# Cross-attention with image prompts: moving the context, prompt-value and input loads from the sync queue to GpSimd's queue

## The chip, the cores and the metric

The kernel runs on one core of a Trainium2 chip. The core has TensorE (PE in the profile) for matrix products, VectorE (DVE), ScalarE (ACT) and GpSimd (POOL) for everything else, and SyncE (SP), which here only issues DMAs. Each engine works through its own queue of instructions in order and meets the others through semaphores. A DMA is started by an instruction in the queue of one of these engines, and the bytes are then moved by 16 DMA engines that the core's queues share. The metric is the time of one execution on the device, in microseconds; a time is a median of several runs.

## What is computed

For each of 8 batch items, 112 positions of 320 channels attend with 20 heads of 16 channels to a context of 375 rows of 512 features. The first 371 rows are text, the last four are image prompts. All data is float32. The reference, cut to what matters:

```python
text_ehs = encoder_hidden_states[:, :-NUM_TOKENS]      # 371 rows
ip_ehs = encoder_hidden_states[:, -NUM_TOKENS:]        # 4 rows
q = heads(hidden_states @ W_q)
k_t = heads(text_ehs @ W_k); v_t = heads(text_ehs @ W_v)
probs_t = softmax(einsum('bhsd,bhtd->bhst', q, k_t) * attn_scale)
text_out = einsum('bhst,bhtd->bhsd', probs_t, v_t)
k_ip = heads(ip_ehs @ W_k_ip); v_ip = heads(ip_ehs @ W_v_ip)
qsem = l2norm(einsum('bhst,bte->bhse', probs_t, text_ehs))
sem = einsum('bhse,bne->bhsn', qsem, l2norm(ip_ehs))
fused = einsum('bhsd,bhnd->bhsn', q, k_ip) * attn_scale + SEM_SCALE * sem
probs_ip = softmax(fused) * spatial_mask[None, None, :, None]
ip_out = einsum('bhsn,bhnd->bhsd', probs_ip, v_ip)
out = (text_out + ip_out) @ W_out + b_out + residual
```

## The kernel before

**Steps and pairs.** The 20 heads of a batch item are five groups of four. A step is one group of one batch item, 40 steps in all. After a prologue the first step runs alone (`alone`), then the steps run two at a time: `pair(n - 1)` multiplies the steps `n - 1` and `n`, and `behind(n)` follows with the projections that later batches need. In the code, `one` and `two` are the two steps of a pair. The last batch has its own ending.

**What a step does.** Scores (L662) go to PSUM; VectorE takes their negated maxima (L675), ScalarE the exponentials `p` (L679) and a copy of the prompts' logits (L681). SyncE's queue sends `p` to the buffer `xg` in four DMAs (L686), one for each head. VectorE transposes `xg` in 32 x 32 blocks into `xgT` (L698), and TensorE multiplies `xgT` with `u` in 12 blocks (L710). `u` holds the Gram matrix of the context beside the values. Its Gram part comes from `ug` by DMAs on SyncE's queue (L488), its value part comes by DMAs through DRAM (L573, L582) to `vr`, and from there by a GpSimd copy for each step and each third of the context (`placed`, L629). VectorE multiplies the products by `p` and sums them (L763). `finish` and its pieces then do the prompts' softmax, the output projection and the store of one batch item, with GpSimd at L809 and L845 to L851.

**Contexts.** A context is transposed by VectorE from `ct` into `ctxT` (L402) in three parts; after the last part GpSimd copies the prompts' four columns in (`prompts_behind`, L390), and the Gram matmuls (L474) read them. `ct` has two buffers, so the context of batch b goes where that of batch b - 2 was. From batch 2 on, `load_ctx` first lets GpSimd clear one block of `ct` (L141); then come four DMAs of 32 x 11 rows of 512 bytes (L143) and four of 19 rows (L148), all on SyncE's queue. `load_next` calls it. It stands at the end of `behind(n)` where the second step of the pair is group 0 of an even batch (loading that batch's number plus 2) or group 4 of an even batch (plus 3).

**Prompt values and inputs.** `prompt_values` (L591) fetches one batch's four value rows from DRAM, repeated over 112 partitions, by one DMA on SyncE's queue. `x` comes in three DMAs on that queue: item 0 in the prologue, items 1 to 4 at L1194 in the first `behind`, items 5 to 7 at L1234 in the second.

**The order.** The order of the work on every engine is written out by hand: an instruction waits behind whatever was emitted before it on its engine. The SyncE queue therefore issues loads, `xg`, `u`, `vr` and `vd` transfers and stores in the order of the code. GpSimd's queue has the copies, clearings and products named above, and, once in the first `behind`, four DMAs (two for `w_out`, one each for the mask and the bias).

Of the kernel before, what the change touches and what calls it, by code (L numbers as in the profile page):

```python
# [20 lines left out]
def kernel(  # L21
# [14 lines left out]
    nc = tc.nc  # L36
# [24 lines left out]
    NG = H // GROUP  # L61
# [73 lines left out]
    def load_ctx(b):  # L135
        ct = io.tile([P, NT, E], F32, tag="ct", name=f"ct_{b}")
        if b >= LEAD:

            v = ct.rearrange("p c e -> p (c e)").rearrange("p (j f) -> p j f", f=P)
            full = TT // RG  # L140
            nc.gpsimd.memset(v[:, full, :], 0.0)  # L141
            for a in range(QN):
                nc.sync.dma_start(  # L143
                    v[a * RG : (a + 1) * RG, :full, :],
                    ehs[b, : full * RG, a * P : (a + 1) * P].rearrange("(j i) f -> i j f", i=RG),
                )
            for a in range(QN):
                nc.sync.dma_start(  # L148
                    v[a * RG : a * RG + TT - full * RG, full, :],
                    ehs[b, full * RG : TT, a * P : (a + 1) * P],  # L150
                )
            return v
        for c in range(NT):
            rows = min(P, T - c * P)
            some = rows - rows % 16
            nc.sync.dma_start(ct[:some, c, :], ehs[b, c * P : c * P + some, :])
            if some < rows:
                nc.sync.dma_start(ct[some:rows, c, :], ehs[b, c * P + some : c * P + rows, :])
        return ct
# [203 lines left out]
    def load_next(b):  # L363
        if 2 <= b < B:
            loaded[b] = load_ctx(b)
# [222 lines left out]

    def prompt_values(b):

        nc.sync.dma_start(  # L591
            st[b]["vip"].rearrange("p n h d -> p (n h d)"),
            vipd[b * NIP : (b + 1) * NIP, :].rearrange("n c -> (n c)").partition_broadcast(S),
        )
# [30 lines left out]
    def placed(b, g, chunks=range(NT)):  # L625

        s = st[b]
        for c in chunks:
            nc.gpsimd.tensor_copy(  # L629
                region(b, c)[:, :, UV - c * P :], s["vr"][:, c * QN : (c + 1) * QN, g, :]  # L630
            )
# [481 lines left out]
    def pair(n):  # L1113

        one, two = steps[n], steps[n + 1]
        b, g = one
        tags = ("mm", "sc") if b % 2 and g == NG - 1 else ("sc", "mm")
        ends = (BLK - 2, BLK - 1)

        products_in(b, g, ("qd",) * GROUP)  # L1120
        for j in range(BLK - 2):
            product(b, g, j, range(GROUP))
            if j < 2:
                heads = (HIGH, LOW)[j]
                coming_scores(n + LEAD, heads, tags[j])
                coming_probabilities(n + LEAD, heads)
            if j == 1:
                transposed(*two, BLK // 2, BLK)
            if j % QN == QN - 1:
                placed(*two, (j // QN,))  # L1130
        products_in(*two, (tags[1],) * 2 + (tags[0],) * 2)
        for there, here in ((HIGH, LOW), (LOW, HIGH)):
            product(*two, 0, there)
            for j in ends:
                product(b, g, j, here)
        del st[b]["xT", g]
        placed(*two, (NT - 1,))
        moved(b, g)
        if g > 1:
            turned(b + 2)  # L1140
        if b % 2 and g in (0, NG - 1):
            f(b - 1 - (g == 0))
        if g in (1, 2):
            f(b - 1, 3 - g)
        reduced(b, g)
        value_sums(b, g)

        b, g = two
        for j in range(1, BLK - 2):
            product(b, g, j, range(GROUP))  # L1150
            if j == 4:
                coming_scores(n + 1 + LEAD, HIGH, "qd")
                coming_probabilities(n + 1 + LEAD, HIGH)
            if j == 7:
                coming_scores(n + 1 + LEAD, LOW, "qd")
                coming_probabilities(n + 1 + LEAD, LOW)
        for heads in (HIGH, LOW):
            for j in ends:
                product(b, g, j, heads)
        del st[b]["xT", g]  # L1160
        moved(b, g)
        if one in ((b, 2), (b, 3)):
            turned(b + 2, 1 + (one == (0, 3)))

    def moved(b, g):

        nb = b + 1
        if b % 2 == 0:
            if g in (1, 2):
                gram_to_groups(nb, (g - 1,))  # L1170
            if g == 3:
                todo = [lambda: gram_to_groups(nb, (3,)), lambda: values_to_groups(nb)]
                for move in reversed(todo) if nb == B - 1 else todo:
                    move()
        else:
            if g in (0, 1):
                gram_to_groups(nb, (g,))
            if g == 2:
                values_to_groups(nb, 0, 2)

    def behind(n):

        b, g = steps[n]
        nb = b + 1
        two = steps[n + 1 : min(n + 3, len(steps) - NG + 1)]

        def tr(i):
            if i < len(two):
                transposed(*two[i], 0, BLK // (1 + i))

        if b % 2 == 0 and g == 0:
            if n == 0:
                turn[:] = ["sc", "mm", "qd", "mm"]
                nc.sync.dma_start(x_sb[:, 1:5, :], x[1:5].rearrange("b s c -> s b c"))  # L1194
            else:
                turn[:] = ["qd"] * 4 + ["mm"]
                k(b)
                f(b - 1)
                if b - 1 < B - 2:
                    prompt_values(b - 1)  # L1200
            if n:
                gr(nb)
            tr(0)
            gr(nb, 2)
            if n:
                f(b - 1)
            else:
                run(("pp",), prompt_projections)
            v(nb)
            tr(1)  # L1210
            if n:
                f(b - 1, 2)
            load_next(b + 2)
            if n == 0:
                load_channels(nc.gpsimd, wo_sb, w_out)
                nc.gpsimd.dma_start(sm_sb, smask.unsqueeze(1))
                nc.gpsimd.dma_start(bias_sb, b_out.partition_broadcast(S))
        elif b % 2 == 0 and g == 2:
            turn[:] = ["qd"] * (6 + (b == 0)) + ["mm"]
            gram_to_groups(nb, (2,))  # L1220
            if b == 0:
                run(("pp",), None)
            k(nb)
            q(nb, 3)
            tr(0)
            v(nb)
            q(nb)
            v(nb)
            if b == 0:
                run(("pp",), None)  # L1230
            tr(1)
            values_to_dram(nb, nc.sync)
            if b == 0:
                nc.sync.dma_start(x_sb[:, 5:, :], x[5:].rearrange("b s c -> s b c"))  # L1234
        elif b % 2 == 0 and nb < B - 1:
            turn[:] = ["qd"] * (4 + (b > 0)) + ["mm", "mm"]
            turned(b + 2)
            q(nb)
            if b > 0:
                f(b - 1)  # L1240
            else:
                run(("t", b), lambda: prompt_logits(b))
            k(nb)
            tr(0)
            if b > 0:
                f(b - 1)
            gr(nb + 1, 3)
            tr(1)
            if b > 0:
                f(b - 1)  # L1250
            load_next(b + 3)
            f(b)
            prompt_values(b)
        elif b % 2 == 0:
            turn[:] = ["qd"] * 4 + ["mm"]
            q(nb, 2)
            f(b - 1)
            k(nb)
            nc.scalar.preload_act_table(AF.Sqrt)
            tr(0)  # L1260
            f(b - 1, 2)
            prompt_values(b)
            f(b, 2)
        elif g == 1:
            turn[:] = ["qd"] * 4 + ["mm"]
            gram_to_groups(nb, (2,))
            q(b)
            k(b)
            k(nb)
            tr(0)  # L1270
            f(b - 1)
            v(nb)
            tr(1)
            v(nb)
            f(b - 1, 3)
            values_to_dram(nb, nc.sync, 0, 2)
            if b == B - 3:
                prompt_values_by_head()
        else:
            turn[:] = ["qd"] * 3 + ["sc"]  # L1280
            v(nb)
            f(b - 1)
            values_to_dram(nb, nc.sync, 2)
            tr(0)
            k(nb)
            f(b - 1, 2)
            tr(1)
            gram_to_groups(nb, (3,))
            values_to_groups(nb, 2)
        assert not turn, (b, g, turn)  # L1290
# [21 lines left out]
    b = B - 1  # L1312
# [116 lines left out]
```

## Time and profile before

| | us |
|---|---|
| runs | 425.0, 419.88, 420.75 |
| median | 420.75 |
| the profiled execution, its own time | 422.32 |
| its span in the profile | 420.6 |

| DMA queue (page of the profile) | packets | MB | share of 16 engines |
|---|---|---|---|
| q1, issued by SyncE | 57054 | 62.32 | 59.1% |
| q0, issued by GpSimd | 192 | 0.55 | 0.7% |

The second table is part 3 of the page. A line of engine groups names the source line, the engine, the operation and "output<-input", then the count, the busy time and the mean of one in ns, and the idle time just before with what ended it. In a timeline a line gives the start and the length in us, and in brackets the idle time before and its releaser. The letters q behind an engine (SPq, POOLq) mean its queue of instructions. In the chain of waits, a line gives the start and length of a stretch of the chain that ended last. In a table of stretches each engine has its busy time and, in brackets, its number of instructions; then come the granted TensorE clock, the DMA share and GB/s. The granted clock of TensorE was 0.997 over this execution.

### The profile page before, as it was taken

To read this page: it belongs to the slowest core of one execution; us is meant where nothing else is said; L and a number is where in the kernel's file an instruction comes from. 1 tells how busy PE (TensorE), PEld (TensorE's weight loads), DVE (VectorE), ACT (ScalarE), POOL (GpSimd) and SP (SyncE) were. 2 spreads that over 40 slices of the span, in tenths; PEclk is the share of its full clock that TensorE was granted. 3 is DMA by queue.
4 is the path that set the end of the run, shared out by engine and by line. 5 is a ranking of instruction groups with operands and counts; after the bars stand their busy time and mean duration, and the time that the engine had idled before them with its cause. 6 is when DMAs were issued, how large, how long until landed. Compare 5 with 4: busy or idle time off the path is not lost.

```text
span 420.6 us, 13818 instructions
## 1 busy us (share of the span) xinstructions
PE 413.4 (98%) x5505; PEld 316.4 (75%) x5505; DVE 322.3 (77%) x685; ACT 185.9 (44%) x634; POOL 115.0 (27%) x277
## 2 busy tenths in 40 slices
PE   8999999999999999999999999999999999999995
PEld 8766686878677786878686877778877878786893
DVE  4055777878888886886888896896887997879975
ACT  3263333324633643424553464333543464346773
POOL 4303310031161342012061235102025136005560
PEclk9999999999999999999999999999999999999998
DMA  8677986778555556577644576575656344676310
GB/s 249 170 195 224 182 168 169 174 183 193 146 160 131 162 137 168 139 166 169 173 122 127 149 172 156 140 171 152 174 136 164 96 121 129 158 167 195 91 42 27
DMA packets 58001, 64.63 MB, mean 154 GB/s; under 512 B 19016, under 2 KB 51760, under 8 KB 57938
## 3 DMA queue, kind: packets, MB, share of 16 engines
q1 hardware_dynamic: 57054, 62.32, 59.1%
q8 instruction: 43, 0.70, 0.8%
q10 hardware_dynamic: 692, 0.89, 0.7%
q0 software_dynamic: 192, 0.55, 0.7%
q14 instruction: 20, 0.16, 0.1%
HBM read 19.04 MB, written 5.22 MB: 58 GB/s over the span
## 4 chain that ended last, share of the span: by engine, by line
PE 91%; DVE 4%; DMA 2%; ACT 1%; POOL 1%; issue 0%; SPq 0%; DVEq 0%; POOLq 0%
PE ps_qd L710 43%; PE ps_v L543 15%; PE ps_k L512 10%; PE ps_g L474 7%; PE ps_s L662 6%; PE ps_q L344 4%; DMA xg<-p 2%; PE ps_o L865 2%; DVE xgT L698 1%; PE ps_g L444 1%; PE ps_c L414 1%; PE ps_w L431 1%; PE ps_kv L280 1%; PE ps_k L503 1%; DVE p L763 1%; POOL shared L752 1%
## 5 line engine op out<-in xcount | busy, mean ns | idle before, releaser
L710 PE MATMUL ps_qd<-u,xgT 32*112 32x40 f32 (+11 forms) x3840 | 217.1, 351 | 1.1 <-DVE ob L871 0.4
L710 PEld LDWEIGHTS ps_qd<-u,xgT 32*112 32x112 f32 x3840 | 179.8, 172 | 38.1 <-issue 6.2
L698 DVE STREAM_TRANSPOSE xgT<-xg 128x768 f32<-128x768 f32 (+1 forms) x63 | 122.9, 1972 | 10.5 <-DMA xg<-p 10.4
L679 ACT ACTIVATE p<-ps_s,nmx 112x371 f32<-112x371 f32 x160 | 85.8, 585 | 61.6 <-DVE nmx L675 61.3
L675 DVE TENSOR_REDUCE nmx<-ps_s 112x1 f32<-112x371 f32 x160 | 77.1, 535 | 34.3 <-PE ps_s L662 32.2
L763 DVE CUSTOM_DVE_ANT_0 p<-ps_qd,p 112x371 f32<-112x371 f32 x150 | 72.5, 539 | 16.5 <-ACT pvs L737 11.1
L629 POOL COPY u<-vr 128x64 f32<-128x64 f32 x120 | 26.8, 237 | 192.3 <-PE ps_qd L710 111.7
L543 PE MATMUL ps_v<-wv_sb,ctxT 128*128 128x384 f32 (+1 forms) x192 | 63.8, 479 | 0.3 <-ACT kT L519 0.3
L662 PE MATMUL ps_s<-kT,qm 32*112 32x375 f32 (+1 forms) x320 | 60.4, 486 | 0.0
L543 PEld LDWEIGHTS ps_v<-wv_sb,ctxT 128*128 128x128 f32 x192 | 35.3, 190 | 21.2 <-ACT kT L519 1.2
L512 PE MATMUL ps_k<-ctxT,wk_sb 128*128 128x371 f32 x136 | 45.8, 481 | 0.0
L737 ACT COPY pvs<-ps_qd 112x21 f32<-112x21 f32 x150 | 21.8, 199 | 52.3 <-DVE ss L763 49.8
L512 PEld LDWEIGHTS ps_k<-ctxT,wk_sb 128*128 128x128 f32 x136 | 24.6, 190 | 13.4 <-ACT ctxT L424 0.5
L474 PE MATMUL ps_g<-ctxT 128*32 128x119 f32 (+11 forms) x672 | 33.3, 344 | 0.0
L474 PEld LDWEIGHTS ps_g<-ctxT 128*32 128x32 f32 x672 | 25.9, 109 | 7.4 <-issue 4.2
L662 PEld LDWEIGHTS ps_s<-kT,qm 32*112 32x112 f32 x320 | 27.2, 171 | 4.8 <-ACT pvs L737 0.5
L550 ACT COPY vext<-ps_v 128x384 f32<-128x384 f32 (+1 forms) x24 | 11.2, 466 | 37.1 <-PE ps_v L543 37.0
L681 ACT COPY ipl<-ps_s 112x4 f32<-112x4 f32 x140 | 24.1, 172 | 0.0
L353 DVE TENSOR_SCALAR qm<-ps_q,emask 128x224 f32<-128x224 f32 (+1 forms) x25 | 8.9, 393 | 17.1 <-PE ps_q L344 17.1
L460 ACT ACTIVATE ug<-ps_g 128x375 f32<-128x375 f32 (+2 forms) x24 | 9.1, 378 | 28.5 <-PE ps_g L474 14.5
L519 ACT COPY kT<-ps_k 128x371 f32<-128x371 f32 x17 | 8.0, 469 | 30.4 <-PE ps_k L512 30.4
L402 DVE STREAM_TRANSPOSE ctxT<-ct 128x512 f32<-128x512 f32 x18 | 19.1, 1066 | 0.0
(158 smaller groups left out, 308.8 us busy)
## 6 DMA issues: line engine op xcount, KB each, us to landing
xg<-p SPq DMA_DIRECT2D x158, 162.3 KB
u<-ug SPq DMA_DIRECT2D x128, 99.0 KB
ct<-in_ctx_dram SPq DMA_DIRECT2D x24, 176.0 KB
vip<-vipd SPq DMA_DIRECT2D x7, 560.0 KB
vr<-vd SPq DMA_DIRECT2D x20, 120.0 KB
vd<-vext SPq DMA_DIRECT2D x14, 160.0 KB
vd<-vext SPq DMA_DIRECT2D x28, 40.0 KB
ct<-in_ctx_dram SPq DMA_DIRECT2D x4, 256.0 KB
```

Of the source, the lines that this page charges most:

```text
L474: nc.tensor.matmul(ps[p * RG : (p + 1) * RG, s0 : T - t0], ctxT[:, e, t0 + q * RG : t0 + (q + 1) * RG], ctxT[:, e, t0 + s0 : T], start=(e ...
L512: nc.tensor.matmul(ps[:, :TT], wk_sb[:, e, i * P : (i + 1) * P], s["ctxT"][:, e, :TT], start=(e == 0), stop=(e == NE - 1),)
L543: nc.tensor.matmul(ps[:, :w], ctxT[:, e, c * P : (c + 1) * P], wv_sb[:, e, :w], start=(e == 0), stop=(e == NE - 1),)
L629: nc.gpsimd.tensor_copy(region(b, c)[:, :, UV - c * P :], s["vr"][:, c * QN : (c + 1) * QN, g, :])
L662: nc.tensor.matmul(ps[:S, :w], qm[a * RG : (a + 1) * RG, i, r, j * S : (j + 1) * S], s["kT"][a * RG : (a + 1) * RG, i, :w], start=True, st ...
L675: nc.vector.tensor_reduce(nmx, ps[:S, :TT], AX.X, ALU.max, negate=True)
L679: nc.scalar.activation(p, ps[:S, :TT], AF.Exp, bias=nmx)
L681: nc.scalar.copy(s["ipl"][:, groups[g][a], :], ps[:S, TT:T])
L698: nc.vector.transpose(xT[:, j : j + n].rearrange("p j (k q) -> p q j k", q=QN), xg[:, :, j * RG : (j + n) * RG].rearrange("p q (j k) -> p ...
L710: nc.tensor.matmul(banks[a][:S, j * RG : UW], xT[a * RG : (a + 1) * RG, j, :S], region(b, c)[a * RG : (a + 1) * RG, p, q * RG :], start=(j ...
L737: nc.scalar.copy(s["pvs"][:, h, :], ps[:S, TT:UW])
L763: nc.vector.tensor_tensor_reduce(out=p, in0=ps[:S, :TT], in1=p, scale=1.0, scalar=0.0, op0=ALU.mult, op1=ALU.add, accum_out=s["ss"][:, h : ...
```

## The change

The eight DMAs of a context from batch 2 on, the prompt values and the x loads after the first item are issued by GpSimd instead of SyncE. `load_next` leaves `behind` and stands within `pair`, between the first step's last products and the second step's remaining ones, right after the third `placed` copy of the second step. The contexts 2, 3, 5 and 7 are thereby issued about half a pair later in the order than before, 4 and 6 earlier: within the pair before the place where they stood. The bytes, their layout and every other instruction stay as they are. The weights, contexts 0 and 1 and the first x item stay on SyncE's queue.

```diff
@@ -140,12 +140,12 @@
             full = TT // RG
             nc.gpsimd.memset(v[:, full, :], 0.0)
             for a in range(QN):
-                nc.sync.dma_start(
+                nc.gpsimd.dma_start(
                     v[a * RG : (a + 1) * RG, :full, :],
                     ehs[b, : full * RG, a * P : (a + 1) * P].rearrange("(j i) f -> i j f", i=RG),
                 )
             for a in range(QN):
-                nc.sync.dma_start(
+                nc.gpsimd.dma_start(
                     v[a * RG : a * RG + TT - full * RG, full, :],
                     ehs[b, full * RG : TT, a * P : (a + 1) * P],
                 )
@@ -588,7 +588,7 @@
     def prompt_values(b):
 
-        nc.sync.dma_start(
+        nc.gpsimd.dma_start(
             st[b]["vip"].rearrange("p n h d -> p (n h d)"),
             vipd[b * NIP : (b + 1) * NIP, :].rearrange("n c -> (n c)").partition_broadcast(S),
         )
@@ -1135,6 +1135,8 @@
                 product(b, g, j, here)
         del st[b]["xT", g]
         placed(*two, (NT - 1,))
+        if (b, g) == (0, 1) or b % 2 and g in (0, NG - 1):
+            load_next(b + 2 + g // (NG - 1))
         moved(b, g)
         if g > 1:
             turned(b + 2)
@@ -1191,7 +1193,7 @@
         if b % 2 == 0 and g == 0:
             if n == 0:
                 turn[:] = ["sc", "mm", "qd", "mm"]
-                nc.sync.dma_start(x_sb[:, 1:5, :], x[1:5].rearrange("b s c -> s b c"))
+                nc.gpsimd.dma_start(x_sb[:, 1:5, :], x[1:5].rearrange("b s c -> s b c"))
             else:
                 turn[:] = ["qd"] * 4 + ["mm"]
                 k(b)
@@ -1210,7 +1212,6 @@
             tr(1)
             if n:
                 f(b - 1, 2)
-            load_next(b + 2)
             if n == 0:
                 load_channels(nc.gpsimd, wo_sb, w_out)
                 nc.gpsimd.dma_start(sm_sb, smask.unsqueeze(1))
@@ -1231,7 +1232,7 @@
             tr(1)
             values_to_dram(nb, nc.sync)
             if b == 0:
-                nc.sync.dma_start(x_sb[:, 5:, :], x[5:].rearrange("b s c -> s b c"))
+                nc.gpsimd.dma_start(x_sb[:, 5:, :], x[5:].rearrange("b s c -> s b c"))
         elif b % 2 == 0 and nb < B - 1:
             turn[:] = ["qd"] * (4 + (b > 0)) + ["mm", "mm"]
             turned(b + 2)
@@ -1248,7 +1249,6 @@
             tr(1)
             if b > 0:
                 f(b - 1)
-            load_next(b + 3)
             f(b)
             prompt_values(b)
         elif b % 2 == 0:
```

## The prediction

> **What bounds the kernel now.** I read the page first, for the busy shares and the chain of work that ended last; then that chain in order of time, for the length of each stretch of the loop; then the timelines of VectorE, SyncE's queue and GpSimd around the context loads.
>
> ```profile
> PE 413.4 (98%) x5505; PEld 316.4 (75%) x5505; DVE 322.3 (77%) x685; ACT 185.9 (44%) x634; POOL 115.0 (27%) x277
> ...
> PE 91%; DVE 4%; DMA 2%; ACT 1%; POOL 1%; issue 0%; SPq 0%; DVEq 0%; POOLq 0%
> ```
>
> TensorE is busy for 98% of the span and makes 91% of the last chain; SyncE's queue makes none of it. So freeing that queue shortens nothing by itself. It can only remove places where TensorE stands still or runs thin because an `xg<-p` transfer came late. The steady loop shows how much there is of that, since every second batch repeats the same work. Pairs of groups begin with ten matmuls of L710:
>
> ```profile
> 89.14 1.15 PE ps_qd L710 x10
> ...
> 110.30 1.15 PE ps_qd L710 x10
> ...
> 167.28 1.15 PE ps_qd L710 x10
> ...
> 188.36 1.15 PE ps_qd L710 x10
> ...
> 208.38 1.15 PE ps_qd L710 x10
> ...
> 265.36 1.15 PE ps_qd L710 x10
> ...
> 307.86 1.15 PE ps_qd L710 x10
> ```
>
> The pair of batch 3, groups 0 and 1, takes 208.38 - 188.36 = 20.02 us. The same pair of batch 1 takes 110.30 - 89.14 = 21.16, which is 1.14 more. From 265.36 to 307.86 there are two pairs in 42.50 us; the same two took 208.38 - 167.28 = 41.10 two batches earlier, so 1.40 is lost there. These 2.5 us are all that the comparison of equal pairs shows to be recoverable. What went wrong stands on VectorE:
>
> ```profile
> 91.02 1.57 DVE L698 STREAM_TRANSPOSE xgT<-xg 128x768 f32<-128x768 f32 x1 [3.04 <-DMA xg<-p]
> ...
> 92.75 1.89 DVE L675 TENSOR_REDUCE nmx<-ps_s 112x1 f32<-112x371 f32 x4
> ...
> 205.37 1.58 DVE L698 STREAM_TRANSPOSE xgT<-xg 128x768 f32<-128x768 f32 x1
> ...
> 209.98 1.89 DVE L675 TENSOR_REDUCE nmx<-ps_s 112x1 f32<-112x371 f32 x4
> ...
> 285.75 1.59 DVE L698 STREAM_TRANSPOSE xgT<-xg 128x768 f32<-128x768 f32 x1 [1.86 <-DMA xg<-p]
> ```
>
> In both slow places VectorE waited for `xg<-p`. The reader should keep one exchange rate from these rows: the maxima (L675) began 92.75 - 89.14 = 3.61 us into the slow pair, and 209.98 - 208.38 = 1.60 into a pair that lost nothing. So 2.0 us of delay on VectorE cost 1.14 on TensorE, and about 0.86 was absorbed.
>
> **Part by part: SyncE's queue.** The change takes 48 context issues, 7 of prompt values and 2 of x off it.
>
> ```profile
> L143 SPq DMA_DIRECT2D ct<-in_ctx_dram x24: 411/465/1696, 43.0 to 284.5; - x24
> L148 SPq DMA_DIRECT2D ct<-in_ctx_dram x24: 224/281/2425, 46.8 to 288.5; - x24
> ```
>
> ```profile
> 183.01 2.05 SPq L143 DMA_DIRECT2D ct<-in_ctx_dram  x4
> 189.46 1.23 SPq L148 DMA_DIRECT2D ct<-in_ctx_dram  x4
> ...
> 191.14 3.54 SPq L686 DMA_DIRECT2D xg<-p  x4
> ...
> 198.86 4.02 SPq L686 DMA_DIRECT2D xg<-p  x4
> ```
>
> By the medians the context issues are 24 x 0.465 + 24 x 0.281 = 17.9 us of that queue, and L148 also holds it until GpSimd has cleared the block (183.01 + 2.05 to 189.46 here). Yet the next `xg<-p` went out only at 191.14, after the last of these at 190.69 and after the prompt values. It follows the probabilities of the pair that began at 188.36, so it has its own reason to be no earlier. I count nothing for the shorter queue here.
>
> At 281.37 it is different: the four `xg<-p` before the load of context 7 had been issued by then, and the transposes could start only at 285.75, 4.4 us later, against 205.37 - 202.88 = 2.5 where no context is on the move.
>
> ```profile
> 277.71 3.66 SPq L686 DMA_DIRECT2D xg<-p  x4
> ```
>
> Context 7 goes out straight behind it. Moving it into the next pair should give back the 1.40. The 1.14 of batch 1 can be due to the queue itself, since in the pair before it one x load is removed:
>
> ```profile
> 73.56 1.56 SPq L1234 DMA_DIRECT2D x_sb<-in_x_dram  x1
> ```
>
> It could give all of 1.14 or nothing; I take half, 0.6. Gains: 2.0 us, between 0 and 2.5.
>
> **GpSimd's queue.** Its own price for an issue has four rows:
>
> ```profile
> L118 POOL DMA_DIRECT2D wo_sb<-in_L_xattn_W_out_dram x1 | 0.9, 918 | 0.0
> ...
> L1216 POOL DMA_DIRECT2D sm_sb<-in_fside_S_dram x1 | 0.6, 554 | 0.0
> L1217 POOL DMA_DIRECT2D bias_sb<-in_L_xattn_b_out_dram x1 | 0.5, 546 | 0.0
> L119 POOL DMA_DIRECT2D wo_sb<-in_L_xattn_W_out_dram x1 | 0.5, 534 | 0.0
> ```
>
> By the code these move 256, 112, 112 and 64 contiguous rows. From 112 rows to 256 the price grows by 0.372 us, 2.6 ns a row. A large context DMA has 32 x 11 = 352 rows, so about 0.918 + 96 x 0.0026 = 1.17 us; a small one has 19 rows, 0.53. An estimate from these rows: 4 x 1.17 + 4 x 0.53 = 6.8 us per context, 7.0 with the clearing. From below it is 8 x 0.53 + 0.2 = 4.4; from above, if all of 918 ns is rows, 352 x 3.6 ns = 1.26 and 7.4. I take 7.0, nearest to the 256-row case. Prompt values cost seven times 0.55 and the two x loads (448 and 336 rows) 1.4 and 1.1. Together 6 x 7.0 + 3.9 + 2.5 = 48 us go onto an engine that has 115.0 busy in 420.6; average room is plenty. What counts is who is queued behind the issues:
>
> ```profile
> 55.01 0.24 POOL L629 COPY u<-vr 128x64 f32<-128x64 f32 x1 [1.30 <-PE ps_qd L710]
> ...
> 132.23 0.24 POOL L629 COPY u<-vr 128x64 f32<-128x64 f32 x1 [2.58 <-DMA vr<-vd]
> 134.39 0.20 POOL L390 COPY ctxT<-ipnT 128x16 f32<-128x16 f32 x1 [1.92 <-DVE ctxT L402]
> ...
> 194.96 0.24 POOL L629 COPY u<-vr 128x64 f32<-128x64 f32 x1 [1.59 <-PE ps_qd L710]
> ...
> 228.85 0.24 POOL L629 COPY u<-vr 128x64 f32<-128x64 f32 x1 [1.15 <-DMA vr<-vd]
> ```
>
> ```profile
> 139.36 4.64 PE ps_g L474 x71
> ...
> 237.44 4.64 PE ps_g L474 x71
> ```
>
> The new place is right behind the third L629 copy of a pair. For contexts 3, 5 and 7 (the place is 195.20 in batch 3) the next three copies and a small one (0.9 us) wait behind the issues, and TensorE needs them at 208.38: room for 12.3 us. For contexts 4 and 6 L390 waits behind them, and the Gram matmuls read its columns: 139.36 - 132.47 - 0.20 leaves 6.7 us, and 237.44 - 229.09 - 0.20 leaves 8.15. So 7.0 us are hidden everywhere but at context 4, which I charge 0.3 us. From above the 7.4 would cost 0.7. The place adds no long wait: the buffer's last reader finished pairs ago, and the prompt values' buffer is freed by GpSimd itself. x is not read before the next pair.
>
> Context 2 is now issued later, from 55.25 to 62.3, and its first reader is L402:
>
> ```profile
> L402 DVE STREAM_TRANSPOSE ctxT<-ct x18: 1005/1056/1127, 74.1 to 330.8; 128x512 f32<-128x512 f32 x18
> ...
> wo_sb<-in_L_xattn_W_out_dram POOLq DMA_DIRECT2D x1, 320.0 KB, 9.9
> ```
>
> Even at 9.9 us to landing it is there at 72.2, ahead of 74.1. The others have at least as long a lead, a full pair.
>
> **The transfers.** The bytes stay, but they move beside other transfers:
>
> ```profile
> 195.00:205.00 10.00, 10.00 (x116) 7.70 (x109) 7.91 (x20) 5.32 (x18) 1.04 (x5) 1.00 0.81 187
> 229.00:237.00 8.00, 8.00 (x177) 7.06 (x170) 6.97 (x17) 3.92 (x17) 0.77 (x4) 1.00 0.36 103
> ```
>
> The last two columns are DMA share and GB/s. A context is 4 x 176 + 4 x 9.5 = 742 KB; at 187 / 0.81 = 231 GB/s it takes 3.2 us of all engines. Around contexts 4 and 6 the share is 0.36, so it fits. Around 3, 5 and 7 only 0.19 x 10 = 1.9 us are free, and 1.3 would push the `xg<-p` of 198.86, whose transposes began at 205.37 with nothing to spare. After the 0.86 that is absorbed, 0.44 remains, three times: 1.3 us. The ends are 0, if `xg<-p` goes first, and 3 x (3.2 - 0.86) = 7.0, if it waits for a whole context.
>
> The Trainium skill (DMA: Bandwidth & Descriptors, Queues, rings and completion order) says that an engine takes turns between the queue rows it has work for, a packet at a time, which speaks against the move: a context on another row no longer stays behind an `xg<-p` issued before it. By it the cost is nearer 7.0 than 0; no row of this trace shows two busy rows side by side for long.
>
> **Sum.** -2.0 + 0.3 + 1.3 = -0.4 us, within 2%. The profiled execution took 422.32 us (span 420.6 and 1.7 around it) and becomes 421.9; the median of the three runs, 420.75, lies 1.6 below it and becomes 420.4.
>
> **The rivals.** First, the loads leave the old places and hurt nowhere: -2.5, 418.2 us. For it speaks that TensorE filled even the stretches at DMA share 0.81; against it, that 205.37 has no spare.
>
> Second, the turns between queues delay `xg<-p` by the whole context in three pairs: +7.0 + 0.3, less up to 1.4, gives 426.7 to 428. For it speaks the exchange rate of batch 1, against it that 2.0 us of lateness cost only 1.14 there. It exceeds 2% only from 8.4 us on, a slip of 3.7 us per context.
>
> Third, on the slower side: GpSimd cannot write its descriptors while VectorE works, and each issue waits out part of a transpose.
>
> ```profile
> L698 DVE STREAM_TRANSPOSE xgT<-xg 128x768 f32<-128x768 f32 (+1 forms) x63 | 122.9, 1972 | 10.5 <-DMA xg<-p 10.4
> ...
> L629 POOL COPY u<-vr 128x64 f32<-128x64 f32 x120 | 26.8, 237 | 192.3 <-PE ps_qd L710 111.7
> ```
>
> At half of 1.97 us for each of eight issues a context takes 14.9 us. Less the rooms, TensorE loses 8.2 and 6.75 at contexts 4 and 6 and 2.6 at each of 3, 5 and 7: 22.8, so 443 us. It decides (2%, 8.4 us) from 11.6 us per context, 1.45 per issue. Against it: the copy at 194.96 and 119 others hold a mean of 237 ns although VectorE is busy 77% of the time, and the four issues took 0.53 to 0.92.
>
> The Trainium skill (SBUF — State Buffer, Who interferes with whom) has the rule: a two-port VectorE copy from SBUF to SBUF locks GpSimd out, and a DMA issued there is starved of descriptors. What VectorE does here in the loop is mostly transposes and reads of PSUM, and the rule names neither, so I give it little.
>
> **How the numbers follow.** Forecast 0.62 (418.7 to 422.5), first rival 0.12, second 0.16, third 0.07; 0.03 is left for a gain over 2% through slack inside TensorE's busy time, which no row shows. Two per cent is about what a measurement of this kernel can tell from no change. Faster by more: 0.03. Slower by more: the third rival and a fifth of the second, 0.10. Within: 0.87. The range goes from below the first rival, 417.8, to the middle of the second, 427; it leaves out about 0.2.
>
> **What would show it.** Right: pairs of batch 3 and batch 5 alike at about 20.0 to 20.5 us, TensorE still near 413 us busy, eight issues on GpSimd in 6 to 8 us right after the third copy, L390 finished just before the Gram matmuls. Wrong: issues of over 1.45 us, TensorE waiting for L390 or L629, or transposes L698 waiting for `xg<-p` by more than 3 us in the pairs with contexts 3, 5 and 7. A time under 412 would mean that the busy TensorE hid stalls that the comparison of pairs does not see.

## The result, and the profile after

| | before | after |
|---|---|---|
| median of 6 runs each, us | 420.56 (419.88 to 425.0) | 434.34 (432.25 to 438.08) |
| span in the profile, us | 420.6 | 433.4 |
| profiled execution, us | 422.32 | 435.55 |

The ratio is 1.0307, with a 95% interval of 1.0273 to 1.0341. The change makes the kernel 3.1% slower; the forecast was 420.4 within 417.8 to 427. Ratios leave out executions in a slower state (two of experiment 2, one of experiment 10).

The page of the changed kernel, parts 1, 3 and 4:

```profile
PE 420.9 (97%) x5505; PEld 319.7 (74%) x5505; DVE 321.5 (74%) x685; ACT 185.7 (43%) x634; POOL 147.0 (34%) x334
...
q1 hardware_dynamic: 46030, 52.74, 49.4%
q0 software_dynamic: 3632, 10.14, 9.5%
...
PE 90%; DVE 3%; DMA 3%; issue 2%; ACT 1%; ACTq 0%; SPq 0%; POOL 0%; DVEq 0%; POOLq 0%
...
L698 DVE STREAM_TRANSPOSE xgT<-xg 128x768 f32<-128x768 f32 (+1 forms) x63 | 122.7, 1972 | 27.5 <-DMA xg<-p 26.7
```

Some 10 MB have gone from SyncE's queue (q1) to GpSimd's (q0), and GpSimd is 32 us busier. TensorE is 7.5 us "busier" with the same 5505 matmuls and no lower a clock, so part of its busy time must be waiting. GpSimd has next to no share in the last chain, so it isn't the new bound. What has grown is the last row: VectorE's transposes now wait 26.7 us for `xg<-p`, against 10.4 before.

The lengths of the pairs say where TensorE pays for it. These are starts of pairs in the chain of waits of the changed kernel, in order of time:

```profile
192.53 1.15 PE ps_qd L710 x10
...
212.55 1.15 PE ps_qd L710 x10
...
232.87 1.15 PE ps_qd L710 x10
...
251.45 1.15 PE ps_qd L710 x10
...
274.14 1.15 PE ps_qd L710 x10
```

The pair from 212.55 takes 20.32 us, where the same pair took 17.89 before. The one from 251.45 takes 22.69 (20.51 before). The other two shown take 20.02 and 18.58, as before. Three kinds of pairs and the ending carry nearly everything, so the rest of the document goes by their sums:

- A: groups 2 and 3 of batches 1, 3 and 5. In the pair ahead of each, context 3, 5 or 7 and the values of an even batch are loaded.
- B: groups 1 and 2 of batches 2, 4 and 6. In the pair ahead of each, the values of an odd batch are loaded, and for the first two context 4 or 6.
- C: groups 0 and 1 of batches 1, 3 and 5, which hold the place of the loads of contexts 3, 5 and 7 in the changed kernel.
- E: the last batch, from its first product with `u` (L710) to its last.

| us | A | B | C | E |
|---|---|---|---|---|
| before | 53.67 | 60.28 | 62.60 | 30.23 |
| after | 60.71 | 66.15 | 60.06 | 31.39 |

So +7.0, +5.9, -2.5 and +1.2; another +1.2 lies ahead of the first pair. Together that is the 12.8 us of the spans. All other pairs agree to 0.1 us. The first pair starts between 48.33 and 51.03 us over the 13 profiles of this study: from 49.50 on in the seven with the contexts on GpSimd, up to 49.45 in the other six. Why is not shown.

One pair of kind A shows the mechanism: the timelines of SyncE's queue, GpSimd and VectorE in the changed kernel.

```profile
202.55 3.76 SPq L686 DMA_DIRECT2D xg<-p  x4
```

```profile
194.21 0.60 POOL L591 DMA_DIRECT2D vip<-vipd  x1
...
199.40 2.49 POOL L143 DMA_DIRECT2D ct<-in_ctx_dram  x4 [0.18 <-issue]
201.88 2.04 POOL L148 DMA_DIRECT2D ct<-in_ctx_dram  x4
203.92 0.58 POOL L629 COPY u<-vr 128x64 f32<-128x64 f32 x3
...
244.68 0.56 POOL L591 DMA_DIRECT2D vip<-vipd  x1
```

```profile
213.50 1.56 DVE L698 STREAM_TRANSPOSE xgT<-xg 128x768 f32<-128x768 f32 x1 [3.86 <-DMA xg<-p]
...
217.45 1.89 DVE L675 TENSOR_REDUCE nmx<-ps_s 112x1 f32<-112x371 f32 x4
...
253.44 1.59 DVE L698 STREAM_TRANSPOSE xgT<-xg 128x768 f32<-128x768 f32 x1 [3.31 <-DMA xg<-p]
```

The context goes out at 199.40, 3.15 us ahead of the four `xg<-p` of 202.55. The last of these is issued by 206.31, but its transpose can start only at 213.50, 7.2 us later; before, the same two rows stood 2.5 us apart. The maxima start 217.45 - 212.55 = 4.90 us into their pair instead of 1.60. They are 3.30 late and TensorE loses 2.43: 0.87 is absorbed, the 0.86 that the prediction had read from batch 1. In the pair of kind B the values go out at 244.68, and the transpose of 253.44 has waited 3.31 us for `xg<-p`.

In each of the six pairs of kinds A and B TensorE stands still once, for 0.4 to 1.2 us, and starts again 1.3 us after the first maxima began: at 257.40 in the pair just named, whose maxima began at 256.11. What they delay is the reading of the scores: ScalarE had read the first of these by 257.29 (L681). The page puts four of these waits, 2.9 us, down to the copy L629, but that had ended by 256.45 here, 0.9 us before TensorE went on; it isn't GpSimd that was late.

The stretches around the pair of kind A, of the changed kernel and then of the one before, where the same place of the pair lies 4.2 us earlier (the last three columns are the granted clock, the DMA share, which can pass 1 a little, and GB/s):

```profile
199.00:204.00 5.00, 5.00 (x96) 4.47 (x89) 3.25 (x10) 2.72 (x11) 4.82 (x11) 1.00 1.04 197
204.00:209.00 5.00, 5.00 (x20) 3.31 (x20) 4.67 (x10) 2.56 (x9) 0.63 (x4) 1.00 1.02 218
```

```profile
197.00:200.00 3.00, 3.00 (x63) 2.92 (x56) 1.99 (x4) 2.21 (x9) 0.61 (x3) 1.00 0.96 201
200.00:203.00 3.00, 3.00 (x14) 2.04 (x13) 2.82 (x10) 0.85 (x7) 0.00 (x0) 1.00 0.57 156
203.00:206.00 3.00, 3.00 (x11) 1.75 (x10) 3.00 (x3) 2.70 (x4) 0.45 (x1) 1.00 0.74 190
```

Up to the `xg<-p` the 16 DMA engines were full before the change too. Behind its start, at 198.86, they had a quarter to two fifths free; in the changed kernel they stay full for all of 10 us. The clock is 1.00 throughout.

### The profile page after: what moved, and what is told of

The parts are those of the page before. It is cut to its first block, busy times and chain, and to the rows that moved or that the text cites. A ratio compares the mean times of both kernels' runs of the same rounds, so it can differ in the third digit from the quotient of the medians.

```text
span 433.4 us, 13820 instructions
## 1 busy us (share of the span) xinstructions
PE 420.9 (97%) x5505; PEld 319.7 (74%) x5505; DVE 321.5 (74%) x685; ACT 185.7 (43%) x634; POOL 147.0 (34%) x334
## 4 chain that ended last, share of the span: by engine, by line
PE 90%; DVE 3%; DMA 3%; issue 2%; ACT 1%; ACTq 0%; SPq 0%; POOL 0%; DVEq 0%; POOLq 0%
PE ps_qd L710 41%; PE ps_v L543 14%; PE ps_k L512 10%; PE ps_g L474 8%; PE ps_s L662 6%; PE ps_q L344 4%; DMA xg<-p 2%; PE ps_o L865 2%; DVE xgT L698 1%; PE ps_g L444 1%; PE ps_c L414 1%; DMA ct<-in_ctx_dram 1%; PE ps_kv L280 1%; DVE nmx L675 1%; PE ps_k L503 1%
## 5 line engine op out<-in xcount | busy, mean ns | idle before, releaser
L710 PE MATMUL ps_qd<-u,xgT 32*112 32x232 f32 (+11 forms) x3840 | 223.8, 352 | 6.4 <-POOL u L629 2.9
L710 PEld LDWEIGHTS ps_qd<-u,xgT 32*112 32x112 f32 x3840 | 182.8, 172 | 46.8 <-issue 8.4
L698 DVE STREAM_TRANSPOSE xgT<-xg 128x768 f32<-128x768 f32 (+1 forms) x63 | 122.7, 1972 | 27.5 <-DMA xg<-p 26.7
L629 POOL COPY u<-vr 128x64 f32<-128x64 f32 x120 | 26.5, 239 | 175.8 <-PE ps_qd L710 111.8
L662 PE MATMUL ps_s<-kT,qm 32*112 32x375 f32 (+1 forms) x320 | 61.6, 486 | 0.0
L681 ACT COPY ipl<-ps_s 112x4 f32<-112x4 f32 x140 | 24.0, 172 | 0.0
L461 POOL TENSOR_TENSOR ug<-ug,half 128x128 f32<-128x128 f32 (+1 forms) x24 | 10.7, 445 | 29.5 <-ACT ug L460 29.5
```

The source lines that it names most:

```text
L629: nc.gpsimd.tensor_copy(region(b, c)[:, :, UV - c * P :], s["vr"][:, c * QN : (c + 1) * QN, g, :])
L662: nc.tensor.matmul(ps[:S, :w], qm[a * RG : (a + 1) * RG, i, r, j * S : (j + 1) * S], s["kT"][a * RG : (a + 1) * RG, i, :w], start=True, st ...
L681: nc.scalar.copy(s["ipl"][:, groups[g][a], :], ps[:S, TT:T])
L698: nc.vector.transpose(xT[:, j : j + n].rearrange("p j (k q) -> p q j k", q=QN), xg[:, :, j * RG : (j + n) * RG].rearrange("p q (j k) -> p ...
L710: nc.tensor.matmul(banks[a][:S, j * RG : UW], xT[a * RG : (a + 1) * RG, j, :S], region(b, c)[a * RG : (a + 1) * RG, p, q * RG :], start=(j ...
```

## The experiments

The times stand beside runs of the kernel before on the same chip: 422.2 (13 runs) for the first four, 421.72 (17) for the next four, 421.63 (16) for the last three.

**1. The change, with the prompt values back on SyncE.**

```diff
 def prompt_values(b):
-    nc.gpsimd.dma_start(
+    nc.sync.dma_start(
```

> The changed kernel, but the prompt values are issued by SyncE again. Theory A: in the pairs of groups 1 and 2 of batches 2, 4 and 6 it is the 560 KB of prompt values, now in flight beside the xg<-p of the pair ahead, that make the second transposes wait (3.31 us of idle before L698 at 253.44). Then these three pairs go back from 22.45, 22.69 and 21.01 us to about 20.5, 20.5 and 19.3, and with up to 1.2 us at the end the time falls by 5.9 to 7.1 us, to about 427 to 428.5. Rival B: contexts 4 and 6, whose issues end at 241.1 shortly before that xg<-p, delay it. Then only the pair of batch 6, which has no context ahead of it, recovers, 1.8 us, and the time is about 432.5.

423.66 us, ratio 1.0028 (1.0003 to 1.0052), below what either theory had. Seven DMAs of 560 KB, some 4 us of GpSimd's time, carry 10.7 of the 13.8 us. B is back at 60.33, as expected; A falls too, to 55.86, which was not. VectorE's wait for `xg<-p` falls from 26.7 to 11.6. What is left in A, 2.2 us, is the contexts' share. One thing moves along with the queue: the values of even batches now go out much earlier, at 183.05 ahead of the pair of 189.01 where GpSimd issued them at 194.21 in the pair of 192.53, which is 7.6 us later in the pair. VectorE in the pair of kind A, and the start of that pair and of the next in the chain:

```profile
207.99 1.56 DVE L698 STREAM_TRANSPOSE xgT<-xg 128x768 f32<-128x768 f32 x1 [1.88 <-DMA xg<-p]
```

```profile
209.01 1.15 PE ps_qd L710 x10
...
227.37 1.15 PE ps_qd L710 x10
```

The wait is 1.88 instead of 3.86, and the pair takes 18.36 instead of 20.32.

**2. The change, with the contexts back on SyncE, at the new place.**

```diff
 (in load_ctx, both loops)
-    nc.gpsimd.dma_start(
+    nc.sync.dma_start(
```

> The changed kernel, but the contexts are issued by SyncE, in the new place; prompt values and x stay with GpSimd. Theory A: what costs time in the pairs of groups 2 and 3 of batches 1, 3 and 5 is that 742 KB are on the move ahead of or beside the second xg<-p of the pair before, whichever queue issues them. On SyncE the context stands in front of it as a whole and its eight issues take about 3 us more of the queue, so these pairs stay at 20 us or above against 17.9, and the time stays within 2 us of 434.3. Rival B: the loss comes from GpSimd's own queue of transfers overtaking SyncE's. Then these three pairs go back to 17.9 us and the time falls by 7.0, to about 427.

444.07 us, ratio 1.0412 (1.0343 to 1.0482), longer than either theory had it. Its span is 436.6, with A 63.69 and B 67.88, worse than the change. SyncE's queue and VectorE in batch 1:

```profile
96.82 2.96 SPq L143 DMA_DIRECT2D ct<-in_ctx_dram  x4
99.88 1.24 SPq L148 DMA_DIRECT2D ct<-in_ctx_dram  x4
101.25 2.60 SPq L488 DMA_DIRECT2D u<-ug  x4
103.95 3.64 SPq L686 DMA_DIRECT2D xg<-p  x4
```

```profile
111.15 1.57 DVE L698 STREAM_TRANSPOSE xgT<-xg 128x768 f32<-128x768 f32 x1 [4.48 <-DMA xg<-p]
```

So it is not GpSimd's queue as such: a context just ahead of `xg<-p` delays it on the same queue too. Whether by its bytes or because `xg<-p` stands behind its issues (they end at 101.12, and `u<-ug` at 103.85) this run doesn't separate; the values are on GpSimd here as well.

**3 and 4. All loads on GpSimd, `load_next` in its old place; and the same with the values on SyncE.**

```diff
 (in pair)
-        if (b, g) == (0, 1) or b % 2 and g in (0, NG - 1):
-            load_next(b + 2 + g // (NG - 1))
 (in behind, where they stood before)
+            load_next(b + 2)
...
+            load_next(b + 3)
 (4 only, in prompt_values)
-        nc.gpsimd.dma_start(
+        nc.sync.dma_start(
```

> The queue part of the change alone: contexts, prompt values and x on GpSimd, load_next back in its old place behind the pair. Theory A: the place costs the pairs of groups 2 and 3 of batches 1, 3 and 5 their 2.1 to 2.5 us each. Here the context goes out after the Gram products, beside the first xg<-p of a pair, whose transposes come half a pair later, so these pairs go back to 17.9 and the time falls by about 7.0, to 427; the prompt values still cost their 5.9. Rival B: any context on GpSimd's queue delays whatever xg<-p is in flight and the loss only moves to the pairs that follow the old place; the time stays at 432 to 436.

> Contexts and x on GpSimd, load_next in its old place, prompt values on SyncE. If both losses are as theory A has them (7.0 us for the place of the odd contexts, 5.9 to 7.1 for the prompt values), nothing is left of the loss and the 2.5 us gained in the pairs of batch 1 and of batches 4 and 5 remain: 418 to 421 us. Rival B: contexts on GpSimd's queue cost time in any place; then it stays above 425.

441.0 us, ratio 1.0441 (1.0371 to 1.0512), and 430.57 us, 1.0204 (1.0155 to 1.0252). Both are far slower than I expected of the old place. With the values, B (69.21) and E (34.15) lose; without them A and B stand where they stood before (53.67 and 60.27), and C alone is long, 67.75 instead of 60.06. GpSimd and TensorE in the fourth kernel:

```profile
193.21 2.57 POOL L143 DMA_DIRECT2D ct<-in_ctx_dram  x4
195.77 2.04 POOL L148 DMA_DIRECT2D ct<-in_ctx_dram  x4
197.82 0.87 POOL L777 TENSOR_TENSOR xb<-x_sb,bias_sb 112x320 f32<-112x320 f32 x1
198.62 0.41 POOL L629 COPY u<-vr 128x64 f32<-128x64 f32 x2
```

```profile
198.92 5.21 PE L710 MATMUL ps_qd<-u,xgT 32*112 32x392 f32 x56 [1.69 <-POOL u L629]
```

On GpSimd's queue the old place is a trap of its own: the eight issues hold back the L629 copies that TensorE needs in the middle of the pair. Two of the three pairs take 22.02 us and the one shown 23.71; in that one the granted clock is 0.66 from 200 to 205 us, so the 1.7 us more are not the wait alone. Issues on GpSimd that hold up TensorE are what the third rival forecast, by another mechanism; the new place behind the third copy avoids this.

**5. The kernel before, with the prompt values alone on GpSimd.**

```diff
 def prompt_values(b):
-    nc.sync.dma_start(
+    nc.gpsimd.dma_start(
```

> The kernel before, with the prompt values alone issued by GpSimd. Theory A: 560 KB on a queue of their own pass the xg<-p that SyncE has issued or is issuing; the pairs of groups 1 and 2 of batches 2, 4 and 6 lose about 1.9 us each as in the changed kernel, and the end about 1: 426 to 430 us. Rival B: the values alone are harmless and only their pile-up with the contexts costs time; then these pairs stay at 20.5, 20.5 and 19.3 us and the time is within 2 us of before.

429.56 us, ratio 1.0171 (1.0113 to 1.0229). B takes 69.06 (before 60.28) and E 31.61; A stays at 53.67. The values of even batches cost nothing by themselves and those of odd batches a great deal. Those of even batches had never stood behind an `xg<-p` of their pair: SyncE issued them at 190.73, ahead of the four of 191.14. For those of odd batches the timelines of all engines show why, against SyncE's queue in the kernel before:

```profile
237.50 3.52 SPq L686 DMA_DIRECT2D xg<-p  x4
...
239.35 0.58 POOL L591 DMA_DIRECT2D vip<-vipd  x1
...
248.85 1.58 DVE L698 STREAM_TRANSPOSE xgT<-xg 128x768 f32<-128x768 f32 x1 [4.11 <-DMA xg<-p]
```

```profile
236.29 3.52 SPq L686 DMA_DIRECT2D xg<-p  x4
239.87 0.54 SPq L591 DMA_DIRECT2D vip<-vipd  x1
240.46 1.93 SPq L143 DMA_DIRECT2D ct<-in_ctx_dram  x4
```

On SyncE the values and context 6 stood behind the four `xg<-p`; the queue kept the order for nothing. On GpSimd the values go out 1.85 us after the first of the four, and the last transposes start 7.8 us after the last issue. The pair that follows takes 24.92 us instead of 20.51. By the exchange rate its maxima, 3.9 us late, account for about 3.0 of the 4.4; in the same pair the granted clock is 0.83 from 250 to 260 us, which the changed kernel doesn't show.

**6. The change, with the values on ScalarE's queue.**

```diff
 def prompt_values(b):
-    nc.gpsimd.dma_start(
+    nc.scalar.dma_start(
```

> The changed kernel with the prompt values on ScalarE's queue. Theory A: any queue other than the one that carries xg<-p will do, because the DMA engines then serve both; the pairs of groups 1 and 2 of batches 2, 4 and 6 stay at 21 us or above and the time at 430 to 437. Rival B: it is GpSimd's own way of issuing (larger packets) that takes the engines; then these pairs go back and the time falls to about 424, as with SyncE.

428.48 us, ratio 1.0168 (1.0135 to 1.0202): between the two theories. The values pass `xg<-p` here too, and sooner, 1.19 us after the first of the four instead of 1.79 in the change. But the wait is 1.00 us instead of 3.31, and B takes 61.96 instead of 66.15; A takes 56.71 instead of 60.71. SyncE's queue, then all engines:

```profile
237.93 15.59 SPq L686 DMA_DIRECT2D xg<-p  x8
```

```profile
239.12 0.32 ACTq L591 DMA_DIRECT2D vip<-vipd  x1
...
246.19 1.59 DVE L698 STREAM_TRANSPOSE xgT<-xg 128x768 f32<-128x768 f32 x1 [1.00 <-DMA xg<-p]
```

So passing `xg<-p` is not the whole price: the queue that the values pass it on counts too.

**7. The contexts alone on GpSimd, at the new place** (experiment 1 with both x loads on SyncE as well).

```diff
-    nc.gpsimd.dma_start(x_sb[:, 1:5, :], ...
+    nc.sync.dma_start(x_sb[:, 1:5, :], ...
```

> Contexts alone on GpSimd, in the new place; prompt values and x on SyncE. Theory A: the 1.14 us gained in the pair of batch 1, groups 0 and 1, come from context 3, which no longer stands beside the xg<-p ahead of that pair; it stays at 20.0 and the time within 1 us of the run with contexts and x on GpSimd (423.7). Rival B: they come from the x load taken off SyncE's queue; then that pair is back at 21.1 us and the time at about 424.8.

424.13 us, ratio 1.0053 (1.003 to 1.0077), A 55.96: the same as experiment 1 within the intervals, and the pair of batch 1 stays at 20.02. So the x loads show no price, and the contexts cost 2.3 us in A. The pair of batch 5 in C takes 21.07 here, 20.02 in experiment 1; experiment 9 says what such a loss is worth.

**8. The kernel before, the values on GpSimd, those of odd batches issued later.**

```diff
 (with the edit of 5; in behind, group 0 of an even batch)
                 f(b - 1)
-                if b - 1 < B - 2:
-                    prompt_values(b - 1)
...
             gr(nb, 2)
+            if n and b - 1 < B - 2:
+                prompt_values(b - 1)
```

> The kernel before, prompt values alone on GpSimd, and for the odd batches issued after the Gram matmuls' doubling on GpSimd instead of before it, some 4 us later, when the xg<-p issued ahead has mostly landed. Theory A: what costs time is overtaking an xg<-p still in flight, so the pairs of groups 1 and 2 of batches 2, 4 and 6 lose less than half of what they lose with the values in the old order on GpSimd, and the time is 421 to 425 us. Rival B: 560 KB on GpSimd's queue cost the same wherever they stand; then the time equals that of the values on GpSimd in the old order, within 1 us.

422.54 us, ratio 1.0019 (0.9996 to 1.0042). B is back at 60.27. All engines, to be set beside the fence of experiment 5:

```profile
234.88 3.52 SPq L686 DMA_DIRECT2D xg<-p  x4
...
241.53 0.57 POOL L591 DMA_DIRECT2D vip<-vipd  x1
241.99 1.55 DVE L698 STREAM_TRANSPOSE xgT<-xg 128x768 f32<-128x768 f32 x1
```

The same DMA on the same queue, now 6.65 us behind the start of the four `xg<-p` instead of 1.85: the transposes don't wait. On a given queue it is the moment that costs.

**9. The kernel before, profiled again.** No edit.

> The kernel before, profiled once more. Theory A: the 1.14 us in the pair of batch 1, groups 0 and 1, and the 1.40 in the pairs of batches 4 and 5 belong to the kernel's order, with context and x on SyncE; both pairs are again at 21.2 and 21.4 us. Rival B: they belong to that one execution, as the runs suggest that keep context and x on SyncE and show 20.02 there; then these pairs are at 20.0 us, or the loss sits somewhere else.

One run, 421.26 us, span 419.6. In batch 1 the pair of kind C, which the prediction gave as slow, takes its 20.02 us, in the chain of waits:

```profile
89.94 1.15 PE ps_qd L710 x10
...
109.96 1.15 PE ps_qd L710 x10
```

C is 60.06 in all, as in the changed kernel. The "recoverable" 2.5 us belonged to one execution, not to the kernel. This profile loses 0.56 us elsewhere, in the pair of batch 2, groups 3 and 4 (21.64 against 21.08). And the pair of batch 5 in C takes 20.70 in experiments 5 and 11, with the contexts on SyncE, 20.78 in 10 and 21.07 in 7, with them on GpSimd: such losses come and go with either queue.

**10. The whole change, with the values of odd batches later** (the edit of 8 within `behind`).

> The whole change, but the prompt values of the odd batches are issued by GpSimd after the doubling of the Gram products. Theory A: those values are the largest part of the loss because they overtake an xg<-p in flight; the pairs of groups 1 and 2 of batches 2, 4 and 6 return to 20.5, 20.5 and 19.3 us, 5.9 us in all, and the time falls to about 427 to 429; what is left are the contexts and the values of the even batches. Rival B: with the contexts on GpSimd as well these bytes cost the same wherever they stand; the time stays above 432.

430.68 us, ratio 1.0188 (1.0139 to 1.0237), somewhat above what theory A had. B recovers in full (60.27); A stays at 59.69. There the values of even batches still meet the contexts.

**11. Experiment 8, with the last batch's values on SyncE.**

```diff
 def prompt_values(b):
+    eng = nc.sync if b == B - 2 else nc.gpsimd
-    nc.gpsimd.dma_start(
+    eng.dma_start(
```

> The kernel before, prompt values on GpSimd with those of the odd batches issued later, and batch 6's values left with SyncE. Theory A: the last values cost the end 1.4 us (31.5 against 30.1 us from the last pair on), which comes back; the time is 420 to 421.5, not above the kernel before. Rival B: the end varies from run to run whatever the values do, and the time equals that of the run in which all values were issued by GpSimd, 422.5.

422.13 us, ratio 1.0016 (0.9987 to 1.0046). E returns from 31.70 to 30.27, so the loss in E is the values of batch 6; the medians alone would not tell the two versions apart. E is 30.1 to 30.3 in all six profiles with these values on SyncE, 30.8 with them on ScalarE's queue, and 31.4 or more in five of the six with them on GpSimd. The sixth is experiment 2 (30.21): there GpSimd issues them 3.35 us after the first of the four `xg<-p`, elsewhere 2.1 to 2.6 us after it. That is the moment again. The time equals that of the kernel before within its interval; no version here beats it.

## Why the prediction was wrong

The step that failed is the one under "The transfers": "The bytes stay, but they move beside other transfers". It then priced the contexts' transfers only. The prompt values had entered the sum as "seven times 0.55", that is as issues on GpSimd, and as nothing else; yet they are 7 x 560 KB, nearly as much as the six contexts, and the kernel before had kept those of the odd batches and of batch 6 behind `xg<-p` by the order of one queue. Of the signs that the prediction named for being wrong, the one that came is transposes waiting for `xg<-p` by more than 3 us.

| term | predicted, us | measured, us | shown by |
|---|---|---|---|
| gains | -2.0 | 0 (-2.5 between the two profiles, but gone without the change too) | 9 |
| values of odd batches | 0 | +5.9 in B | 1, 5, 8, 10 |
| values of batch 6 | 0 | +1.2 in E | 2, 5, 11 |
| contexts | +1.3 | +2.2 alone | 1, 7 |
| values of even batches | 0 | 0 alone; with the contexts A is +7.0 (+6.0 in 10), so +4.8 (+3.8) on top of their 2.2 | 1, 5, 10 |
| issues on GpSimd | +0.3 | none seen in A, B, C or E | 1, 7 |
| ahead of the first pair | 0 | +1.2, cause open | - |
| x loads | 0 | 0 | 7 |

The point on the even batches deserves care. In A the values alone cost nothing and the contexts alone 2.2; together, with the DMA engines full for 10 us, they cost 7.0. How the two add up is not shown: the values of 194.21 landed after 5.2 us, just when the context went out, and experiment 1 changed their moment along with their queue. The prediction's upper end, for contexts that `xg<-p` waits out whole, was 7.0 as well; that is chance, since the contexts alone cost 2.2.

The second rival, "the turns between queues", was right in kind: loads on another queue delay an `xg<-p` issued before them. Its price was not: at 426.7 to 428 it charged whole contexts, and the values, in A, B and E, are a carrier that it didn't name. The rule of the Trainium skill quoted there (DMA: Bandwidth & Descriptors, Queues, rings and completion order) pointed the right way; that the engines take turns packet by packet no run here shows.

**Gains.** The two slow places had been read out of one execution by comparing equal pairs. The second profile of the same kernel doesn't have them. That C fell to 60.06 with the change is therefore no success of the forecast.

**SyncE's queue.** Right: freeing it shortened nothing by itself. Its order, though, had been worth something, and the prediction didn't ask what would pass what once it was gone.

**GpSimd's queue.** Cover and place were right. GpSimd is 32 us busier, where the prediction had 48: by the medians a context's eight issues took 4.6 us, not 7.0, near the lower bound of 4.4:

```profile
L143 POOL DMA_DIRECT2D ct<-in_ctx_dram x24: 625/628/684, 56.8 to 304.0; - x24
L148 POOL DMA_DIRECT2D ct<-in_ctx_dram x24: 505/518/539, 59.3 to 306.1; - x24
```

The price by rows was wrong: 352 rows of a context cost 628 ns and 19 rows 518, and the x loads took 0.93 and 0.75 us instead of 1.4 and 1.1. All 48 lie between 505 and 684, so none waits out a transpose and the third rival's mechanism isn't there. That issues ahead of the L629 copies cost time is real, as experiment 4 shows for the old place: 4.6 us of them cost 2.0 us in two of three pairs and 3.7 in the third, at its lower clock.

**The exchange rate.** Right: in the changed kernel the maxima of A are 3.0 to 3.3 us late and those of B 2.7 to 3.1, and 0.87 to 0.96 of that is absorbed in each of the six pairs.

**Left open.** The slip is longer than the bytes need. In experiment 5 the last transposes start 7.8 us after the last issue, 5.3 more than the usual 2.5, for one DMA of 560 KB, which at the prediction's 231 GB/s fills all engines for 2.4. The DMA view, in windows of 10 us around the values, for experiments 5, 6 and 8 in turn (queue, packets, MB, share of 16 engines):

```profile
q1 hardware_dynamic: 1471, 1.14, 64.2%
q0 software_dynamic: 128, 0.57, 33.5%
```

```profile
q1 hardware_dynamic: 614, 0.79, 33.1%
q10 hardware_dynamic: 128, 0.57, 22.0%
```

```profile
q1 hardware_dynamic: 1487, 1.12, 47.7%
q0 software_dynamic: 128, 0.57, 20.7%
```

The same 128 packets hold the engines for 3.35 us beside `xg<-p` on GpSimd's queue, and for 2.20 and 2.07 on ScalarE's and when later; the packets of q1 take longer in the first case than in the third as well (64.2% against 47.7% for nearly the same bytes). Experiment 6 has its contexts on GpSimd, so its fair partner is the change: there the values' queue takes 28.8% for 0.59 MB and q1 34.0% for 0.77 MB. Taking turns by packets, with 4.5 KB in each of the values' and 0.8 KB in each of q1's, would explain a delay beyond the bytes' share, but the packets of ScalarE's queue are as large and cost a wait of 1.00 us instead of 3.31. The runs don't settle it.

## What to carry to other kernels

A queue that isn't on the critical path may still be worth its order: before moving a bulk load to another queue, look for the small transfer that it stood behind, and at who waits for that. Price each moved DMA twice, by its issue on the new engine and by its bytes beside the transfers it may now pass, and add up the loads that meet at one moment, since two that cost little alone (0 and 2.2 us in A) cost 7.0 together here. A gain read from the differences between equal stretches of one profile needs a second profile before it enters a sum.

## What the runs showed of the hardware

Moving seven transfers of 560 KB from SyncE's queue to GpSimd's, with nothing else changed, cost 1.7% (1.1 to 2.3, experiment 5). The Trainium skill (DMA: Bandwidth & Descriptors, Issuing engines are not separate DMA queues) says that transfers interleave on the same DMA engines whoever starts them, and that another engine saves only the time to start them. The interleaving agrees with the late transposes; that the choice of queue saves little is true here, but it can lose far more: 7.8 us of the median, some 1.4 of it in a pair with a lower clock, for seven issues of 0.3 to 0.5 us that SyncE was spared. And the time of an issue on GpSimd doesn't go by the number of rows alone. In the changed kernel it was 518 ns for 19 rows of a context, 560 to 610 for the 112 of the values and 628 for 352 of a context, but 782 for the 256 of `w_out` and 930 for the 448 of the first x load.
